# Turning the last batch of a GRU stream by VectorE and an exchange on GpSimd's queue, and moving one split behind the last sum

## The chip, the core and the metric

The kernel runs on one NeuronCore of one Trainium2 chip. The metric is the device time of one execution in microseconds (us), as the median of several runs; lower is better. The engines are TensorE (PE in the profile, its weight loads PEld), VectorE (DVE), ScalarE (ACT), GpSimd (POOL) and SyncE (SP). SyncE and GpSimd also issue transfers; each engine works off its own queue in order.

## The reference

The input is 16 graphs (batches) of 1024 nodes with 128 features, `x`, and a 0/1 adjacency matrix for each, `adj`. Two layers follow each other, each with a residual:

```python
h = jnp.maximum(_layernorm(x), 0.0)
for i in range(4):                                  # layer 0: gated
    hw = einsum('bnc,cd->bnd', h, weight[i])
    m = einsum('bjn,bjd->bnd', adj, hw)             # sum over neighbours
    h = _gru_cell(m, h, w_ih[i], w_hh[i], b_ih[i], b_hh[i])
x = x + h * mask
h = jnp.maximum(_layernorm(x), 0.0)
for i in range(4):                                  # layer 1: convolutions
    h = relu(einsum('bnm,bmc->bnc', adj, h @ W[i]) + b[i])
    mu, var = mean and variance of h over all batches and nodes
    h = gamma[i] * (h - mu) * rsqrt(var + EPS) + beta[i]
x = x + h
```

The GRU cell forms r and z with a sigmoid, n = tanh(xn + r * hn), and h = (1 - z) * n + z * h.

## The kernel before, in words

**Layout.** A batch is cut into eight blocks of 128 nodes and, for the gates, into two halves of 512 nodes. The gates work with features on the partitions (tile h, 128 x 1024). The sum over neighbours wants nodes on the partitions, split into a high part[...] and the low rest (two tiles, ghw in layer 0, chw in layer 1), so that each sum is done with two products for each row block (`aggregate_rows`, L520 to L530: 8 blocks x 2 parts x 2 halves = 32 products of 512 columns).

**Layer 0.** Two streams run against each other: `sa` does the even batches, `sb` the odd ones. In a half step (`half_step`, L1095) one stream does its sum over neighbours on TensorE while the other does its gates on ScalarE and VectorE. The order in this layer is written out by hand for every engine until the last half step; the calls under L1283 keep it by hand for TensorE, GpSimd and SyncE alone, and the rest, layer 1 included, is put in order by a scheduler that lets instructions of the two layers mix on each queue. After a sum, `agg_rows` (L947) copies the two halves from PSUM to the tiles m on ScalarE (L955, remembered as `last_m`); then `products` (L976, L993) does the gate products, `reset_gate`, `candidate` and `update_gate` the ScalarE and VectorE part, `less` and `mixed` the last of h (L1029, L1033, L1034).

**From features to nodes.** Between steps h is turned from features to nodes on the partitions in two moves: VectorE transposes 32 x 32 blocks (`half_out`, L719, into a tile t_h or t_out), and an exchange through DRAM puts the blocks where they belong (`exchange_out`, L588; `exchange_in`, L594; `pair_in`, L600, for both halves at once). The transfers go on SyncE's queue. `half_away` (L891) does this for each half as soon as it is ready. At the end of a batch (i + 1 - hf == L) it does so only if its stream has another batch (`self.b + 2 < B`), and `finish` (L1039) then fetches the pair back into the old h tile.

**The last two batches.** Batch 14 (stream sa) and batch 15 (stream sb) have no successor. `finish` calls `last_tail` (L757), and `tail_sums` (L726) turns h by eight transposes on TensorE (L735, tile pt_x), then adds it to x with the mask on VectorE (L741, one instruction for each block) and takes the statistics of the second layer norm (L664, L665). `last_tail` stores x (xmid, L752) on GpSimd's queue; its `rest` later normalizes (L680, y_mid) and stores that (ymid, L755). For batch 14 that is called after the last gates of batch 15, for batch 15 in the first convolution.

**Layer 1, first convolution.** `load_adjT` (L1303) brings the transposed adjacency of a batch from DRAM on SyncE's queue, as bfloat16 (L1308: tile block for even batches, packed for odd ones), and widens it to the rows wide (L1311 ScalarE for blocks 1, 4 and 7, L1313 VectorE for the others). `first_split` (L1366) loads y of a batch on GpSimd's queue (L1368), copies it to the high part on ScalarE (L1370) and subtracts for the low part on VectorE (L1371). The high and low tiles of even batches use the same memory as ghw of stream sa, those of odd batches that of stream sb, so a split waits for the last sum that read them. The sums of even batches are pc_m, of odd ones pc_g_r and pc_g_z. `row_sums` (L1402, pt_deg) counts neighbours once for batch 0, and `first_weights` (L1374, pw) applies the weight to a finished sum. `fetch_x` (L1426) brings part of x back early into weight tiles that are no longer used (w_hhT, w_mT), on GpSimd's queue too.

Of the kernel before, what the change touches and what calls it, by code (L numbers as in the profile page):

```python
# [17 lines left out]
HALF = 512  # L18
# [323 lines left out]
def exact_path(  # L342
# [21 lines left out]
    nc = tc.nc  # L364
    B, N, C = x.shape
    L = g_weight.shape[0]
    NB = N // P
    NH = N // HALF
# [13 lines left out]
    def tmp(name):  # L382
        return ps_t.tile([P, HALF], F32, tag="tmp", name=name)
# [5 lines left out]
    def flat(name):  # L389
        return keep.tile([P, NB, C], F32, tag="x", name=name, bufs=4)  # L390
# [4 lines left out]
    def half_tile(name):  # L395
        return keep.tile([P, N], BF16, tag="half", name=name, bufs=8)
# [4 lines left out]
    def hw_tiles(b, name):  # L401
        return [keep.tile([P, N], F32R, tag=f"hw{b % 2}{s}", name=f"{name}_{s}") for s in range(2)]
# [61 lines left out]
    turned = {}  # L464
# [68 lines left out]
    with ExitStack() as st:  # L533
# [51 lines left out]
                k = b * NB + j  # L585
                nc.scalar.activation(junk, lows, AF.Copy, accum_out=low[:, k : k + 1])

        def exchange_out(t, name, d=None):  # L588
            if d is None:
                d = rawd.tile([P, HALF], F32, tag="cross", name=f"cross_{name}", bufs=8)  # L590
            nc.sync.dma_start(d, t)
            return d

        def exchange_in(d, t):  # L594
# [2 lines left out]
            for s in range(4):  # L597
                nc.sync.dma_start(t[s * 32 : (s + 1) * 32, :].rearrange("r (t x) -> r t x", t=4), src[s])

        def pair_in(d, t):  # L600

            src = d.rearrange("h (t r) (s x) -> s r (h t) x", t=4, s=4)
            for s in range(4):
                nc.sync.dma_start(t[s * 32 : (s + 1) * 32, :].rearrange("r (a x) -> r a x", a=8), src[s])

        def look(b, row, j, part=0):

# [76 lines left out]
        def norm_stats(xt, name):  # L684
            nt = norm_tiles(name)
            norm_sums(xt, nt, range(NB))
            return nt

        def norm_apply(xt, y, nt):
            norm_root(nt, 0, NB)  # L690
            norm_scale(nt, 0, NB)
            norm_blocks(xt, y, nt, range(NB))
# [13 lines left out]
        def by_nodes(cols):  # L706
            return cols.rearrange("c (q k i) -> c k q i", q=4, i=32)

        def four_ways(cols):
            return cols.rearrange("p (k a c) -> p k a c", a=4, c=32)  # L710

        def blocks_out(src, name):

            d = rawd.tile([NH, P, HALF], F32, tag="pair", name=f"pair_{name}", bufs=4)
            for hf in range(NH):
                half_out(cross_tile(f"t_{name}_{hf}"), src, hf, name, d[hf])
            return d

        def half_out(t, src, hf, name, d=None):  # L719
            turned = nc.vector.transpose(by_nodes(t), four_ways(src[:, hf * HALF : (hf + 1) * HALF]))  # L720
            return exchange_out(t, f"{name}_{hf}", d), turned

        def cross_tile(name):
            return half_tile(name).bitcast(F32)

        def tail_sums(b, xt, hT, parts=None):  # L726

            for hf in range(NH):
                if parts:
                    pt = by_nodes(parts[hf])  # L730
                else:
                    pt = tmp(f"pt_x{b}_{hf}")
                    for q in range(BH):
                        k = hf * BH + q
                        nc.tensor.transpose(pt[:, q * P : (q + 1) * P], hT[:, k * P : (k + 1) * P], ident)  # L735
                    pt = four_ways(pt)
                for q in range(BH):
                    k = hf * BH + q
                    xk = xt[:, k, :].rearrange("p (a c) -> p a c", a=4)
                    mask = maskT[:, b * NB + k : b * NB + k + 1]  # L740
                    nc.vector.scalar_tensor_tensor(xk, pt[:, q, :, :], mask, xk, ALU.mult, ALU.add)  # L741
            return norm_stats(xt, f"mid{b}")
# [5 lines left out]
        def y_mid(b):  # L748
            return work.tile([P, N], F32, tag="h", name=f"y_mid{b}", bufs=7)

        def store_xmid(b, xt):
            nc.gpsimd.dma_start(xmid_d[b].rearrange("(k p) c -> p k c", p=P), xt)  # L752

        def store_ymid(b, y):
            nc.gpsimd.dma_start(ymid_d[b], y)  # L755

        def last_tail(b, xt, hT):  # L757
            nt = tail_sums(b, xt, hT)
            y = y_mid(b) if b + 1 < B else xt.rearrange("p k c -> p (k c)")
            store_xmid(b, xt)  # L760

            def rest():
                norm_apply(xt, y, nt)
                store_ymid(b, y)

            return rest
# [3 lines left out]
        class Stream:  # L770
# [119 lines left out]

            def half_away(self, hf):  # L891

                if self.i + 1 - hf == L and self.b + 2 < B:
                    if hf == 0:
                        self.pair = rawd.tile([NH, P, HALF], F32, tag="pair", name=f"pair_out{self.b}", bufs=4)
                    half_out(cross_tile(f"t_out{self.b}_{hf}"), self.new, hf, f"out{self.b}", self.pair[hf])
                elif self.turned_away(self.i + 1 - hf):
                    nm = f"{self.b}_{self.i + 1 - hf}"
                    out, self.last_dve = half_out(cross_tile(f"t_h{nm}_{hf}"), self.new, hf, f"h{nm}")
                    self.outs.append(out)  # L900
# [138 lines left out]
            def finish(self):  # L1039

                if self.i < L:
                    return
                args = self.b, self.xt, self.hT
                self.b, self.i = self.b + 2, 0
                if self.b >= B:
                    self.rest = last_tail(*args)
                    return
                self.take()
                ins, outs, h_in = self.next_ins, self.pair, self.hT
                parts = [args[-1][:, hf * HALF : (hf + 1) * HALF] for hf in range(NH)]  # L1050

                last = args[-1]
                at(clock[0] + 1, "ins", lambda: pair_in(ins, h_in))
                at(clock[0] + 1, "outs", lambda: pair_in(outs, last))
                self.plan(clock[0], (*args, parts))
# [3 lines left out]
        def at(n, place, go):  # L1059
            agenda.setdefault((n, place), []).append(go)  # L1060
# [91 lines left out]
        sa, sb = Stream(0), Stream(1)  # L1152
# [188 lines left out]
    def conv_input(b, i, aff, parts=1):  # L1341
        hT = work.tile([P, N], F32, tag="h", name=f"bn{b}_{i}", bufs=3)
        for k in range(parts):
            cols = slice(k * N // parts, (k + 1) * N // parts)
            nc.scalar.activation(hT[:, cols], feat[b][:, cols], AF.Identity, bias=aff[1], scale=aff[0])
        return hT

    def conv_hw(b, i, hT):
        hw = hw_tiles(b, f"chw{b}_{i}")
        for g in range(NH):  # L1350
            features_times(w_c[:, i, :], hT, hw, g, f"c{b}_{i}")
        return hw
# [13 lines left out]
    def first_split(b):  # L1366
        yt = flat(f"y{b}").rearrange("p k c -> p (k c)")
        nc.gpsimd.dma_start(yt, ymid_d[b])  # L1368
        hw = hw_tiles(b, f"chw{b}_0")
        nc.scalar.copy(hw[0], yt)  # L1370
        nc.vector.tensor_sub(hw[1], yt, hw[0].bitcast(F32))  # L1371
        return hw

# [76 lines left out]

    stats = small.tile([P, B * NH, 6], F32, tag="bn_st", name="stats0")
    hw, waiting = first_split(0), None
    for b in range(B):
        rows = load_adjT(b, 0)
        hw_next = first_split(b + 1) if b + 1 < B else None
        pm = banks(b, 0)
        aggregate(pm, hw, rows, 0)
        if waiting:
            last = first_weights(*waiting, stats)
            if b == 1:  # L1460
                with tc.issue_after(last.ins):
                    sb.rest()
        if b == B - 1:
            hw_next = raw_split(1)
        aggregate(pm, hw, rows, 1)
        if b == 0:
            row_sums(rows)
        hw, waiting = hw_next, (b, pm)
# [3 lines left out]
    for i in range(1, L):  # L1472
# [7 lines left out]
        hw = conv_hw(1, i, conv_input(1, i, aff, 2))  # L1480
        aggregate_rows(pm0, hw0, rows, range(6, NB))
        for b in range(1, B):
# [19 lines left out]
            hw = hw_next  # L1502
# [9 lines left out]
    for b in range(B):  # L1512
        hT = work.tile([P, N], F32, tag="h", name=f"bn{b}_{L}", bufs=3)
# [69 lines left out]
```

## Time and profile before

| what | value |
|---|---|
| median of 3 runs (lowest, highest) | 1788.07 us (1785.47, 1794.2) |
| the profiled execution's own time | 1789.26 us |
| its span, first to last instruction | 1787.5 us |
| TensorE busy, matmuls | 1759.3 us (98%) |
| VectorE, ScalarE, GpSimd busy | 1305.9, 1107.6, 379.3 us |
| granted TensorE clock, mean | 0.999 |
| gates of batch 14 on TensorE | 1137.25 to 1147.77 us |
| sum of batch 15 on TensorE | 1147.77 to 1155.47 us |
| transposes and gates of batch 15 | 1155.47 to 1166.64 us |
| first convolution, batch 0 | 1166.64 to 1175.17 us |
| batch 1, with row sums and weights | 1175.17 to 1188.12 us |

The times within the span count from its first instruction. A line of the timeline gives start, duration, engine, source line, operation, tile written and tiles read, shape and number of instructions, and in brackets how long the engine was idle before it and what ended that. Matmuls overlap in the pipeline, so the difference of two starts says more of TensorE's pace than the duration does: 0.23 us for a product of 512 columns with a high or low part, 0.86 us for two passes of a gate product.

### The profile page before, as it was taken

To read this page: it belongs to the slowest core of one execution; us is meant where nothing else is said; L and a number is where in the kernel's file an instruction comes from. 1 tells how busy PE (TensorE), PEld (TensorE's weight loads), DVE (VectorE), ACT (ScalarE), POOL (GpSimd) and SP (SyncE) were. 2 spreads that over 40 slices of the span, in tenths; PEclk is the share of its full clock that TensorE was granted. 3 is DMA by queue.
4 is the path that set the end of the run, shared out by engine and by line. 5 is a ranking of instruction groups with operands and counts; after the bars stand their busy time and mean duration, and the time that the engine had idled before them with its cause. 6 is when DMAs were issued, how large, how long until landed. Compare 5 with 4: busy or idle time off the path is not lost. (4 is left out here: it accounts for less than half of the span.)

```text
span 1787.5 us, 22335 instructions
## 1 busy us (share of the span) xinstructions
PE 1759.3 (98%) x6734; PEld 1191.7 (67%) x6734; DVE 1305.9 (73%) x2310; ACT 1107.6 (62%) x1713; POOL 379.3 (21%) x417
## 2 busy tenths in 40 slices
PE   9999999999999999999999999999999999999997
PEld 6565655565656565556555556577778888888886
DVE  7677877887887787887797787676666666666665
ACT  5356556556566556665655655476777767768765
POOL 4314323332331331422432333010100000000011
PEclk9999999999999999999999999999999999999999
DMA  7467657777676676776756768788766575767667
GB/s 259 135 175 262 189 163 272 179 208 241 204 200 213 223 212 197 245 202 202 260 169 186 265 174 227 256 287 311 271 228 241 207 253 201 245 224 245 238 217 268
DMA packets 363617, 400.16 MB, mean 224 GB/s; under 512 B 158188, under 2 KB 239888, under 8 KB 363488
## 3 DMA queue, kind: packets, MB, share of 16 engines
q1 hardware_dynamic: 342736, 323.59, 57.6%
q0 software_dynamic: 20224, 74.80, 11.3%
q8 instruction: 55, 0.90, 0.2%
q14 instruction: 74, 0.61, 0.1%
q10 hardware_dynamic: 528, 0.26, 0.0%
HBM read 267.47 MB, written 97.52 MB: 204 GB/s over the span
## 5 line engine op out<-in xcount | busy, mean ns | idle before, releaser
L524 PE MATMUL pm<-row,ghw 128*128 128x512 f32 x2048 | 503.6, 402 | 0.7 <-DVE ghw L926 0.6
L524 PEld LDWEIGHTS pm<-row,ghw 128*128 128x128 f32 x2048 | 383.8, 188 | 106.6 <-issue 29.2
L1016 ACT ACTIVATE r<-r,vecs 128x512 f32<-128x512 f32 x128 | 92.6, 723 | 255.0 <-DVE r L1013 253.1
L524 PE MATMUL pc_m<-wide,chw 128*128 128x512 f32 x1024 | 245.3, 395 | 0.0
L615 POOL CAST half<-row 128x1024 bf16<-128x1024 f32 x128 | 147.4, 1161 | 361.1 <-DMA adjT<-half 347.9
L524 PEld LDWEIGHTS pc_m<-wide,chw 128*128 128x128 f32 x1024 | 190.4, 188 | 41.9 <-issue 3.8
L524 PE MATMUL pc_g_r<-wide,chw 128*128 128x512 f32 x464 | 186.9, 403 | 0.3 <-ACT chw L501 0.3
L524 PE MATMUL pc_g_z<-wide,chw 128*128 128x512 f32 x464 | 181.0, 390 | 0.0
L577 POOL CAST row<-stage 128x1024 fp32r<-128x1024 f32 x112 | 128.6, 1156 | 243.7 <-DMA stage<-in_adj_dram 232.2
L1012 DVE SCALAR_TENSOR_TENSOR r<-g_hn,vecs,r 128x512 f32<-128x512 f32 x128 | 93.3, 729 | 117.9 <-ACT r L1011 66.9
L955 ACT COPY m<-pm 128x512 f32<-128x512 f32 x128 | 68.4, 585 | 163.5 <-PE pm L524 163.5
L1313 DVE CAST wide<-block 128x1024 fp32r<-128x1024 bf16 x160 | 109.9, 692 | 75.5 <-PE pc_m L524 48.3
L1313 DVE CAST wide<-packed 128x1024 fp32r<-128x1024 bf16 x160 | 110.1, 691 | 71.9 <-PE pc_g_z L524 53.5
L1311 ACT CAST wide<-packed 128x1024 fp32r<-128x1024 bf16 x96 | 100.6, 1048 | 58.5 <-PE pc_m L524 29.7
L993 PE MATMUL g_r<-m,w_mT 128*128 128x512 f32 x256 | 132.0, 597 | 3.4 <-ACT m L955 2.9
L1311 ACT CAST wide<-block 128x1024 fp32r<-128x1024 bf16 x96 | 100.7, 1049 | 53.9 <-PE pc_g_z L524 27.7
L993 PE MATMUL g_z<-m,w_mT 128*128 128x512 f32 x256 | 130.7, 592 | 0.0
L993 PE MATMUL g_xn<-m,w_mT 128*128 128x512 f32 x256 | 130.7, 592 | 0.0
L1361 DVE BATCH_NORM_STATS2 stats<-feat 128x6 f32<-128x512 f32 x128 | 84.1, 686 | 47.0 <-ACT feat L1360 45.9
L1029 DVE TENSOR_TENSOR h<-h,r 128x512 f32<-128x512 f32 x96 | 83.8, 872 | 41.9 <-ACT r L1016 41.8
L1033 DVE TENSOR_TENSOR h<-h,z 128x512 f32<-128x512 f32 x128 | 107.8, 842 | 6.8 <-ACT z L1020 0.2
L1011 ACT ACTIVATE r<-g_r,brz 128x512 f32<-128x512 f32 x128 | 87.9, 686 | 39.1 <-PE g_r L993 38.8
(186 smaller groups left out, 2830.5 us busy)
## 6 DMA issues: line engine op xcount, KB each, us to landing
block<-adjT_d SPq DMA_DIRECT2D x256, 256.0 KB, 4.7
packed<-adjT_d SPq DMA_DIRECT2D x256, 256.0 KB, 5.5
stage<-in_adj_dram SPq DMA_DIRECT2D x120, 512.0 KB, 5.7
adjT_d<-adjT POOLq DMA_DIRECT2D x16, 2048.0 KB, 7.7
cross_h<-t_h SPq DMA_DIRECT2D x92, 256.0 KB, 2.2
n_h<-cross_h SPq DMA_DIRECT2D x368, 64.0 KB, 2.0
xmid_d<-x POOLq DMA_DIRECT2D x16, 512.0 KB, 6.9
y<-ymid_d POOLq DMA_DIRECT2D x16, 512.0 KB, 5.4
```

The source lines that it names most:

```text
L524: nc.tensor.matmul(pm[hf], hw[s][:, j * P : (j + 1) * P], rows[j][:, hf * HALF : (hf + 1) * HALF], start=(j == 0 and s == 0), stop=(j == N ...
L577: nc.gpsimd.tensor_copy(t, stage[j % 4])
L615: nc.gpsimd.tensor_copy(t, row.bitcast(F32))
L993: nc.tensor.matmul(po, wT[:, i, g * C : (g + 1) * C], rhs, start=start, stop=stop)
L1011: nc.scalar.activation(r, pr, AF.Sigmoid, bias=brz[:, 3 * i : 3 * i + 1])
L1012: nc.vector.scalar_tensor_tensor(r, phn, b_hn(i), r, ALU.add, ALU.mult)
L1016: nc.scalar.activation(self.r, self.r, AF.Tanh, bias=b_in(self.i))
L1029: nc.vector.tensor_sub(ho, hin, self.r)
L1033: nc.vector.tensor_mul(ho, ho, self.z)
L1311: nc.scalar.copy(r, t)
L1313: nc.vector.tensor_copy(r, t)
L1361: nc.vector.bn_stats(stats[:, b * NH + hf, :], dst)
```

## The change

There are two edits, both at the passage from layer 0 to layer 1.

First, `half_away` also turns the two halves of the last batch of stream sa (batch 14) by VectorE, into t_out, and sends them to DRAM, on GpSimd's queue. `last_tail` of that stream then fetches them back into the h tile with four transfers, on GpSimd's queue too, and `tail_sums` adds from that tile in place of a PSUM tile, so that the eight transposes of batch 14 on TensorE are no longer made. Batch 15 stays as it was.

Second, the copy of the high part in `first_split` is put into `tc.issue_after(sb.last_m.ins)`: the scheduler may not place it before the last copy of m of stream sb (batch 15). It bears on the batches 0 and 1, whose copies would otherwise come earlier.

```diff
-        def exchange_out(t, name, d=None):
+        def exchange_out(t, name, d=None, eng=nc.sync):
...
-            nc.sync.dma_start(d, t)
+            eng.dma_start(d, t)
...
-        def pair_in(d, t):
+        def pair_in(d, t, eng=nc.sync):
...
-                nc.sync.dma_start(t[s * 32 : (s + 1) * 32, :].rearrange("r (a x) -> r a x", a=8), src[s])
+                eng.dma_start(t[s * 32 : (s + 1) * 32, :].rearrange("r (a x) -> r a x", a=8), src[s])
...
-        def half_out(t, src, hf, name, d=None):
+        def half_out(t, src, hf, name, d=None, eng=nc.sync):
...
-            return exchange_out(t, f"{name}_{hf}", d), turned
+            return exchange_out(t, f"{name}_{hf}", d, eng), turned
...
-        def last_tail(b, xt, hT):
-            nt = tail_sums(b, xt, hT)
+        def last_tail(b, xt, hT, outs=None):
+            parts = None
+            if outs is not None:
+                pair_in(outs, hT, nc.gpsimd)
+                parts = [hT[:, hf * HALF : (hf + 1) * HALF] for hf in range(NH)]
+            nt = tail_sums(b, xt, hT, parts)
...
-                if self.i + 1 - hf == L and self.b + 2 < B:
+                if self.i + 1 - hf == L and (self.b + 2 < B or self is sa):
+                    eng = nc.sync if self.b + 2 < B else nc.gpsimd
...
-                    half_out(cross_tile(f"t_out{self.b}_{hf}"), self.new, hf, f"out{self.b}", self.pair[hf])
+                    half_out(cross_tile(f"t_out{self.b}_{hf}"), self.new, hf, f"out{self.b}", self.pair[hf], eng)
...
-                    self.rest = last_tail(*args)
+                    self.rest = last_tail(*args, self.pair if self is sa else None)
...
-        nc.scalar.copy(hw[0], yt)
+        with tc.issue_after(sb.last_m.ins):
+            nc.scalar.copy(hw[0], yt)
```

In the changed program as built, TensorE's queue has eight instructions fewer (pt_x14), GpSimd's has six transfers more (two stores of t_out, four loads of h), and VectorE's has two transposes more. The copies of chw of the batches 0 and 1 stand on ScalarE behind the copies of m of batch 15. The scheduler has also put other things in another order: on SyncE, two transfers of the second block tile now come before the eight of packed; on ScalarE, the copy of chw of batch 2 now comes before the eight instructions y_mid of batch 14; on TensorE, the sixteen products of the row sums come after batch 1's sum and no longer in its middle, and the transposes of batch 15 stand some products later in batch 0's sum.

## The prediction, made before the changed kernel was run

> **What bounds the kernel now.** I read the page first. TensorE is busy in all but 28 us of the span of 1787.5 us, so only what makes TensorE's queue shorter, or makes it wait, can move the end.
>
> ```profile
> PE 1759.3 (98%) x6734; PEld 1191.7 (67%) x6734; DVE 1305.9 (73%) x2310; ACT 1107.6 (62%) x1713; POOL 379.3 (21%) x417
> ```
>
> Next the waits of TensorE alone (total us, times, longest): none is large, but one is what the last edit addresses, a gate product waiting for the copy of a sum out of PSUM.
>
> ```profile
> PE g_z L993 <- ACT z L1020: 5.0, 8, 0.7
> ...
> PE g_r L993 <- ACT m L955: 2.9, 4, 1.0
> ```
>
> All that the diff touches runs at one place, the passage from the first layer to the second, 1130 to 1190 us; the order of the changed program, as built, differs elsewhere by only one exchange of two neighbours (below). So I read the timelines there (start, duration, engine, line). TensorE:
>
> ```profile
> 1137.25 1.02 PE L993 MATMUL g_r<-h,w_hhT 128*128 128x512 f32 x2
> 1138.62 1.13 PE L993 MATMUL g_r<-m,w_mT 128*128 128x512 f32 x2 [0.34 <-ACT m L955]
> 1139.58 1.02 PE L993 MATMUL g_hn<-h,w_hhT 128*128 128x512 f32 x2
> ...
> 1155.47 1.03 PE L735 MATMUL pt_x<-ident,h 128*128 128x128 f32 x8
> 1156.34 1.02 PE L993 MATMUL g_r<-h,w_hhT 128*128 128x512 f32 x2
> ...
> 1166.64 0.60 PE L735 MATMUL pt_x<-ident,h 128*128 128x128 f32 x4
> 1166.99 3.46 PE L524 MATMUL pc_m<-wide,chw 128*128 128x512 f32 x14
> ```
>
> The reader is to see that TensorE is gapless but for 0.34 us, and that the eight transposes of batch 14 take 0.87 us of its queue (1155.47 to 1156.34). ScalarE shows why the gap is there: the copy of chw (batch 0) was let go before the copies of m and ran first.
>
> ```profile
> 1137.04 1.05 ACT L1370 CAST chw<-y 128x1024 fp32r<-128x1024 f32 x1 [6.04 <-PE pm L524]
> 1137.99 1.07 ACT L955 COPY m<-pm 128x512 f32<-128x512 f32 x2
> ...
> 1170.38 3.19 ACT L680 ACTIVATE y_mid<-x,ms_mid,rs_mid 128x128 f32<-128x128 f32 x8 [0.94 <-DVE ms_mid L676]
> 1174.92 1.05 ACT L1370 CAST chw<-y 128x1024 fp32r<-128x1024 f32 x1 [1.34 <-PE pc_m L524]
> 1176.28 1.05 ACT L1311 CAST wide<-packed 128x1024 fp32r<-128x1024 bf16 x1 [0.30 <-PE pc_g_z L524]
> ```
>
> Last, SyncE's queue and the table of transfers (us to landing): packed goes out before the second block.
>
> ```profile
> 1144.45 6.62 SPq L1308 DMA_DIRECT2D packed<-adjT_d  x8
> 1152.56 4.59 SPq L1308 DMA_DIRECT2D block<-adjT_d  x8
> ```
> ```profile
> pair_out<-t_out SPq DMA_DIRECT2D x28, 256.0 KB, 5.2
> ...
> h<-pair_out SPq DMA_DIRECT2D x56, 128.0 KB, 4.5
> ```
>
> [...]
>
> **The change part by part.** Negative is time won.
>
> (1) chw of batch 0 behind the last m. The product that read m started 1.37 us after the one before it (1137.25 to 1138.62), the next 0.96 later; the pace without a wait is 0.86. That is 0.51 + 0.10: **-0.61**. The two copies now run on ScalarE after m of batch 15, some 1156.0 to 1158.0; first user is the convolution's product after 1165, so this is covered, unless by what follows in (3).
>
> (2) The pt_x14 transposes go: **-0.87**. Added on VectorE are two t_out of 0.71; removed before them is the low part of chw (1.22), which moves later. The eight sums for x14 now read SBUF: 37.6 us over 112 is 0.34 each, 2.7 for eight, against 2.3 from PSUM (4.6 over 16).
>
> (3) VectorE's queue ahead of batch 15's last gates. As built, SyncE now issues two transfers of the second block before packed, and they wait until block's last casts are done (about 1152.2, as before, when 1152.56 was that wait). Packed 0 so goes out at 1153.2 instead of 1144.45, with two of 256 KB ahead of it; I take its landing as 1157, four us after issue as for the first block (1140.42 to the cast at 1144.52), bounds 1156 and 1159. VectorE, with t_out out of the way by 1153.9, stands at the cast of packed 0 till then. Behind it in order: that cast 0.60, chw low of two batches 2 x 1.2, scalar_tensor_tensor 0.65, cast 0.60, add 0.60: 1161.9. Tanh 0.7 on ScalarE, then h-r, h*z, the second scalar_tensor_tensor (1.9 together): 1164.6. Eight sums of x14 2.7, a statistic 0.2, h+r 0.6: h of the first half is ready at 1168.1. TensorE, 1.48 us ahead of the old time, starts the convolution at 1165.16, does seven products at 0.2275 and comes to pt_x15 at 1166.75: it **waits 1.35**. Then transposes 0.45, sixteen products 3.64, to 1172.2; the second half's add, tanh, and three operations with statistics between end about then. Transposes 0.45, nine products 2.05, the flag 0.15: batch 0 ends at 1174.85. The stage lasted 8.53 (1166.64 to 1175.17) and lasts 9.69: **+1.16**. Bounds -0.3 (no wait) and +3.2 (packed at 1159).
>
> (4) ScalarE's queue after it. As built, chw of batch 2 now stands before the eight y_mid and wide 4 behind them; before, y_mid was done while ScalarE would have waited. Chw 2 waits for batch 0's last high product, about 1174.4; +1.05, +3.19, +1.05: wide 4 is ready at 1179.7. TensorE wants it after sixteen products, 1174.85 + 3.64 = 1178.5: **waits 1.2**. The row sums that before stood in the middle of that batch (16 products, 3.75) now follow it, so nothing fills the gap. Thirty-two products 7.28, row sums 3.75, two weight products 1.71, and 1.2: 13.94 against 12.95 before (1175.17 to 1188.12): **+0.99**. Bounds 0 and +2.
>
> (5) The exchange itself, on GpSimd's queue. Two stores of 0.55 issue each, four loads of about 0.6 (between the 0.55 of a load of 128 rows and the 0.91 of one with 1024 pieces), then y2, y3 and x14's store queued behind. Second t_out at 1153.9; store landed after 3.3 (rows: 2.8 to 8.3 for w_hhT in this stretch): 1157.2; last load issued 1.8 later, landing 4.5 (pair_out's row): 1163.5. VectorE asks at 1164.6: covered, **0**. Y2 then lands near 1166, wanted at 1174.4; y3 and the x store have more room. Packed 6 and 7 wait for the two stores, since they share buffers; they are wanted after 1178. Bound above: 8.3 for the store is +4 after that cover.
>
> (6) At the second convolution four products (hw_c2) trade places with two of batch 1: nothing is removed, 0; bounds 0.3 either way, the only wait of a product on ScalarE's chw in TensorE's list.
>
> Sum: -0.61 - 0.87 + 1.16 + 0.99 = **+0.7 us**. The profiled execution took 1789.26 (span plus 1.76 around it), so 1789.9 on its own; on the median of the runs, 1788.07, it is **1788.7**. From 1188 us on TensorE has no gap, so what is won or lost there stays to the end.
>
> **Rivals.** *Faster*: packed lands by 1156 and ScalarE's order costs nothing; then only (1) and (2) count, with up to 0.5 of idle that the old stages had: -1.5 to -2.0, 1786.3. For it: VectorE was idle 0.6 at 1155.5 and the DMA share fell to 0.77 just before. Against: the order in (4) is fixed in the program. *Slower*: the exchange lands late. VectorE stands in order at x14's first sum, behind it h+r, behind that TensorE's pt_x15. It decides from 1164.6 on; each us later adds one. With store 5.2 and loads 4.5 plus 1.8 it lands at 1165.4; with the store at 8.3, at 1168.5: +0.8 to +4 more, so 1789.5 to 1793; I take 1791.5. For it: the pieces are 512 bytes and share the DMA engines with block and packed, which filled them (share 0.93 to 1.04 in these stages). *No effect as said*: ruled out for both edits by the order as built. An order elsewhere that hurts: left as 0.04.
>
> **How the numbers follow.** Main case 0.50; faster 0.23; exchange late 0.23; something else, either sign, 0.04. The runs before spread from 1785.47 to 1794.2, wider than any case, and a bound of 0.5% (8.9 us) is about what a measurement of this kernel can tell from no change. The range takes in both rivals but for the outer end of the slow one: 1785.2 to 1792.8. All three cases lie within 0.5%, so same 0.95; faster 0.02, slower 0.03 are the rest, as the late exchange has no bound in the rows but needs 8 us past its cover.
>
> **What would show it.** In the changed profile: no "ACT m" wait before the product at 1138 and the next step 0.86 after it; no pt_x<-h of batch 14; VectorE idle until "DMA packed" near 1154 to 1157; TensorE idle at pt_x15 on h (about 1.3) and at the fifth row of batch 1 on "ACT wide" (about 1.2); no VectorE idle before x14's sums. I am wrong if TensorE passes either place without waiting, or if VectorE waits there for h<-pair_out.

## The result, and the profile after

The changed kernel takes 1803.45 us in the median of 5 runs (1801.01 to 1804.12), the kernel before, beside it, 1789.79 us (5 runs, 1785.47 to 1794.2): a ratio of 1.0067, 95% interval 1.0054 to 1.0079. The forecast was 1788.7, its range ended at 1792.8. The profiled execution took 1803.86 us, its span is 1802.0.

The page first. TensorE has eight instructions fewer and 2.4 us more of busy time; the mean granted clock is 0.995, before it was 0.999.

```profile
PE 1761.7 (98%) x6726; PEld 1191.7 (66%) x6726; DVE 1300.5 (72%) x2312; ACT 1107.3 (61%) x1713; POOL 381.8 (21%) x423
```

TensorE's waits (total us, times, longest). The three lines are new: none of them is in the profile before. Each happens once, and all lie in the passage between the layers.

```profile
PE pt_x L735 <- DVE h L1039: 7.7, 1, 7.7
PE pc_g_r L524 <- ACT wide L1316: 1.1, 1, 1.1
PE pt_deg L1413 <- DVE ones_r L1454: 0.7, 1, 0.7
```

TensorE's timeline there:

```profile
1167.13 1.02 PE L998 MATMUL g_z<-m,w_mT 128*128 128x512 f32 x2
1167.59 2.16 PE L524 MATMUL pc_m<-wide,chw 128*128 128x512 f32 x7
1177.42 1.11 PE L735 MATMUL pt_x<-ident,h 128*128 128x128 f32 x4 [7.68 <-DVE h L1039]
1178.19 6.27 PE L524 MATMUL pc_m<-wide,chw 128*128 128x512 f32 x16
...
1192.04 0.50 PE L524 MATMUL pc_g_r<-wide,chw 128*128 128x512 f32 x1 [1.12 <-ACT wide L1316]
...
1196.66 3.92 PE L1413 MATMUL pt_deg<-wide,ones_r 128*128 128x512 f32 x16 [0.65 <-DVE ones_r L1454]
```

TensorE does its seven products as forecast and then stands for 7.68 us, not 1.35, at batch 15's first transposes. The sixteen products after that take 6.27 us; at the pace of the kernel before (0.23 us for each) they would take about 3.8. The next view, windows of the same trace (PEclk is the column before the last two), tells why: the clock fell to half while TensorE stood (at 1173.0, 3.3 us after its last product), and stayed there after it went on.

```profile
1166.20:1174.40 8.20, 3.54 (x12) 1.89 (x10) 1.45 (x4) 0.69 (x1) 2.17 (x4) 0.92 1.01 297
1174.40:1177.42 3.02, 0.00 (x0) 0.00 (x0) 3.02 (x12) 0.00 (x0) 0.55 (x1) 0.50 1.04 416
1177.42:1182.00 4.58, 4.58 (x13) 3.80 (x14) 4.50 (x19) 2.00 (x2) 0.36 (x1) 0.50 0.66 255
```

TensorE waited for h, h for VectorE. VectorE's queue shows two stops, the first at packed, the second at the first sum of batch 14. The timeline names no releaser for the second, the view of the tile pair_out below does:

```profile
1155.66 0.71 DVE L720 STREAM_TRANSPOSE t_out<-h 128x512 f32<-128x512 f32 x1
1159.98 0.69 DVE L1318 CAST wide<-packed 128x1024 fp32r<-128x1024 bf16 x1 [3.60 <-DMA packed<-adjT_d]
...
1166.92 0.74 DVE L1017 SCALAR_TENSOR_TENSOR r<-g_hn,vecs,r 128x512 f32<-128x512 f32 x1
1174.39 2.19 DVE L741 SCALAR_TENSOR_TENSOR x<-h,maskT,x 128x128 f32<-128x128 f32 x8 [6.72 <-issue]
```

What it waited for is on GpSimd's queue: the second store of the exchange, the four loads behind it. The view of the tile pair_out from 1155 us on then gives who waited for these five transfers, and their time from issue to landing.

```profile
1156.67 0.54 POOL L591 DMA_DIRECT2D pair_out<-t_out  x1 [5.86 <-DVE t_out L720]
1163.47 2.70 POOL L604 DMA_DIRECT2D h<-pair_out  x4 [6.27 <-DMA pair_out<-t_out]
```
```profile
  DVE x L741: 6.7, 1
...
DMA to landing us min/median/max: 5.7/6.1/8.6
```

The store landed 6.1 us after its issue, at about 1162.8; the loads after 5.7 to 8.6, the last at about 1174.2; VectorE went on at 1174.39. SyncE meanwhile kept the DMA engines full (DMA share 1.01 and 1.04 in the windows above) with transfers of 256 KB:

```profile
1155.22 7.94 SPq L1313 DMA_DIRECT2D packed<-adjT_d  x8
1163.21 2.80 SPq L1313 DMA_DIRECT2D block<-adjT_d  x6
```

**A ruler.** The median of the kernel before moves by a few us from run to run, with nothing different in the passage. So beside every median I give the *stretch*, from the start of the last pair of gate products g_z of layer 0 to the end of TensorE's last product, in the profiled execution. It is 612.0 us before and 624.7 after: +12.7. The waits make 7.68 + 1.12 + 0.65 = 9.45 of it. The clock, half from the restart at 1177.42 to about 1183.3, costs half of 5.8 us, 2.9. That is 12.4 of the 12.7. What steps (1) and (2) won lies ahead of the stretch.

### The profile page after: what moved, and what is told of

Its sections match the earlier page's. It is cut to its first block, busy times and chain, and to the rows that moved or that the text cites. A ratio compares the mean times of both kernels' runs of the same rounds, so it can differ in the third digit from the quotient of the medians.

```text
span 1802.0 us, 22329 instructions
## 1 busy us (share of the span) xinstructions
PE 1761.7 (98%) x6726; PEld 1191.7 (66%) x6726; DVE 1300.5 (72%) x2312; ACT 1107.3 (61%) x1713; POOL 381.8 (21%) x423
```

## The experiments

Two theories. **T1**: the exchange costs everything; it lands late, TensorE stands, and the clock falls. **T2**: the moved copy and the new queue orders ((3), (4)) cost most. Every kernel was timed beside the kernel before. "Ratio" is against that kernel on the same chip, with its 95% interval (it is taken from the single runs and isn't exactly the quotient of the two medians); the diffs are against the changed kernel unless said otherwise.

| run | median us (before) | ratio | stretch, change | TensorE's waits in the passage, us |
|---|---|---|---|---|
| e1_exchange_only | 1803.17 (1790.34) | 1.0069 [1.0053, 1.0086] | +9.6 | 5.8, 1.1, 0.2 |
| e2_copy_only | 1790.27 (1790.34) | 0.9998 [0.9988, 1.0008] | +0.1 | 0.2 |
| e3_on_sync | 1793.22 (1790.34) | 1.002 [1.0012, 1.0029] | +3.8 | 1.1, 2.15 |
| e4_sums_behind_gates | 1800.48 (1790.34) | 1.0056 [1.0038, 1.0074] | +9.7 | 1.6, 5.2 |
| e10_no_wait | 1796.75 (1791.21) | 1.0025 [1.0012, 1.0037] | +4.0 | 0.3, 1.1, 2.1 |
| e5_packed_first | 1798.55 (1791.21) | 1.003 [1.0018, 1.0042] | +8.5 | 3.9, 1.1, 0.6 |
| e6_idle72 | 1806.72 (1791.21) | 1.0079 [1.0062, 1.0095] | +16.1 | 1.1, 3.2, 0.2 |
| e9_sync_no_late | 1794.94 (1791.21) | 1.0018 [1.001, 1.0027] | +3.0 | 2.8 |
| e11_in_place | 1792.77 (1791.1) | 1.0006 [0.9996, 1.0015] | 0.0 | none |
| e12_crowd_held | 1797.43 (1791.1) | 1.0041 [1.0027, 1.0055] | +7.0 | 1.1, 3.7 |
| e13_held_in_place | 1794.68 (1791.06) | 1.0022 [1.0012, 1.0031] | +4.7 | 2.8 |
| e14_in_place_again | 1790.98 (1791.06) | 0.9999 [0.9988, 1.0009] | +0.1 | 0.15 |

### Each edit alone: e1_exchange_only, e2_copy_only

The first leaves out the second edit; the second kernel is the one before with the second edit alone.

```diff
-        with tc.issue_after(sb.last_m.ins):
-            nc.scalar.copy(hw[0], yt)
+        nc.scalar.copy(hw[0], yt)
```

> Only the first edit (batch 14 by VectorE and the exchange on GpSimd's queue); the copy of chw is left where the kernel before has it. T1 (the late exchange holds up VectorE's queue, in which the sums of batch 14 stand ahead of gates of batch 15): in this build the sums stand ahead of the second half's h-r and no longer ahead of the first half's h+r, so the long wait of TensorE moves from the first to the second pt_x of batch 15; with the transfer landing near 1174 us and the second half's last three gate steps of about 4 us behind the sums, TensorE waits 6 to 10 us there and its granted clock falls after it: 1798 to 1804 us. T2 (the loss comes from the second edit and the order that it gives to ScalarE): 1787 to 1791 us, no wait of TensorE above 2 us.

> Only the second edit (chw's copy behind the last m); batch 14 is turned by TensorE as before. T1: nothing is left to be late, so -0.6 us for the copy that no longer stands ahead of m, and the mean within noise of the kernel before: 1787 to 1791 us, no wait of TensorE above 1.5 us in the passage. T2: the loss stays, 1799 to 1805 us.

The first edit alone costs what the change costs, the copy alone nothing that can be measured. In e1_exchange_only TensorE waits 5.78 us for h at the *second* half's transposes, and the granted clock is 0.50 from 1176.8 to 1183.65. Its stretch doesn't hold all of its loss: batch 15's gates, just ahead, take 11.4 us from the first product to the last g_z, against 9.4 before, with waits for m and r. The copy is cleared, but the queue orders are not: e1_exchange_only has both of them (VectorE waits 4.31 us for packed, TensorE 1.08 for wide), e2_copy_only neither, so they come with the exchange. How much of the loss is the late landing and how much the orders, the next runs have to tell.

### The same exchange on SyncE's queue: e3_on_sync

```diff
-                pair_in(outs, hT, nc.gpsimd)
+                pair_in(outs, hT)
...
-                    eng = nc.sync if self.b + 2 < B else nc.gpsimd
+                    eng = nc.sync
```

> The changed kernel with batch 14's exchange on SyncE's queue, as all the other batches have it. In this build the sums of batch 14 stand on VectorE ahead of the second half's h-r of batch 15, and the four loads stand on SyncE behind packed 0 to 3. T1 with GpSimd's queue as the cause of the lateness: the loads land by about 1165 us, before VectorE asks, and the time is 1787 to 1791 us. T1 with the crowd of transfers as the cause: they land at 1170 to 1174 us on this queue too, TensorE waits 4 to 9 us at the second pt_x of batch 15: 1793 to 1802 us. T2: 1799 to 1805 us whatever the landing.

The view of pair_out gives the four loads' time to landing, and TensorE's and VectorE's timelines what is left:

```profile
DMA to landing us min/median/max: 3.5/3.5/3.5
```
```profile
1178.27 0.50 PE L524 MATMUL pc_g_r<-wide,chw 128*128 128x512 f32 x1 [1.12 <-ACT wide L1316]
1183.90 3.88 PE L1413 MATMUL pt_deg<-wide,ones_r 128*128 128x512 f32 x16 [2.15 <-DVE ones_r L1454]
```
```profile
1183.58 0.23 DVE L1454 CAST ones_r<-ones 128x128 fp32r<-128x128 f32 x1 [3.31 <-DMA ymid_d<-y_mid]
```

The exchange is over at 1160.8, 3.8 us before VectorE's first sum (1164.54); the 7.7 us are gone, with the clock's fall. But two waits stay, and the time lies between the two cases of the expectation. The first wait is step (4)'s. The second was in nobody's sum: ones_r is a constant that reads no y, yet it waits until the store of batch 14's y has landed, which points to memory that it takes over from y (e11_in_place tests that). Batch 14's sums and the store of its y, in the kernel before and then here:

```profile
1156.10 2.16 DVE L741 SCALAR_TENSOR_TENSOR x<-pt_x,maskT,x 128x128 f32<-128x128 f32 x8 [0.60 <-PE pt_x L735]
1173.87 0.54 POOL L755 DMA_DIRECT2D ymid_d<-y_mid  x1 [6.23 <-ACT y_mid L680]
```
```profile
1164.54 2.18 DVE L741 SCALAR_TENSOR_TENSOR x<-h,maskT,x 128x128 f32<-128x128 f32 x8
1177.57 0.54 POOL L755 DMA_DIRECT2D ymid_d<-y_mid  x1
```

The sums start 0.8 us after the last g_z here (1163.70) and started 9.7 us before it in the kernel before (1165.78). So y is stored 13.9 us after that product, before 8.1; the store also takes 5.9 us to land, before 2.9; and what takes y's memory next is held up. I call this the **second chain**.

### VectorE not held by the sums: e4_sums_behind_gates

Batch 14's sums get their place behind the last gates of batch 15.

```diff
...
+            with tc.issue_after(sb.last_dve.ins):
+                rest = sa.rest()
             with tc.issue_after(sb.last_act.ins):
-                sa.rest()
+                rest()
```

> The changed kernel with the sums of batch 14 (x + h) kept on VectorE's queue behind the last gate step of batch 15; the exchange stays as late as it is. T1: TensorE's wait at the first pt_x of batch 15 falls from 7.7 to under 1.5 us and the clock stays up; of the loss of 13.7 us, 6 to 12 come back, the rest is a new wait of batch 1's sum for rows that VectorE widens behind batch 14's sums and statistics: 1790 to 1797 us. T2: nothing comes back, 1801 to 1805 us.

Missed: the transposes no longer wait, but y is later still, ones_r waits for its store, and TensorE stands 5.21 us before the row sums, which then take 6.17 us for sixteen at half the clock (0.50 from 1182.3 to 1189.1). The loss has moved from the first chain to the second.

### Nothing waits for the loads: e10_no_wait

All six transfers stay, but the loads go to a tile of their own, and the sums of batch 14 take h as it stands, with features where nodes belong: this kernel leaves batch 14's turning out of its result. The sums stay behind the second r of batch 15 by hand, but the scheduler now puts the last step of h of the first half ahead of them.

```diff
-                pair_in(outs, hT, nc.gpsimd)
+                pair_in(outs, y_mid(100), nc.gpsimd)
...
```

> The changed kernel with every transfer as it is, but the four loads land in a spare tile and the sums of batch 14 take h as it stands (features where nodes belong: batch 14's rows of the result are other ones), so that VectorE has no landing to wait for; the eight sums stand at the same place in its queue, behind the second r of batch 15. T1: the loss goes with the wait, no wait of TensorE above 1.5 us at the transposes of batch 15 and no fall of its clock: 1788 to 1791 us. T2 (order of ScalarE and SyncE) or a cost of the transfers' traffic by itself: the loss stays in part or whole, 1794 to 1803 us.

In between. TensorE's waits:

```profile
PE pt_deg L1419 <- DVE ones_r L1460: 2.1, 1, 2.1
PE pc_g_r L524 <- ACT wide L1322: 1.1, 1, 1.1
```

So the wait for the loads, with its clock and the place of the sums, carries 12.7 - 4.0 = 8.7 us of the stretch. Of the 4.0 that stay, 3.5 are the three waits in the table (0.3, 1.1 and 2.1), so the transfers going by cost at most half a us beside them; and e3's two waits are back, whichever queue the exchange is on. VectorE waits 3.44 us for packed here too, and TensorE no more than 0.27 at the transposes.

### packed before block: e5_packed_first

SyncE's order is put back as it was, so that VectorE doesn't wait for packed (step (3)).

```diff
...
+            if b == 2 and i == 0:
+                with tc.issue_after(sent[-1].ins):
+                    nc.sync.dma_start(t, adjT_d[b][j])
+            else:
+                sent.append(nc.sync.dma_start(t, adjT_d[b][j]))
```

> The changed kernel with one constraint on SyncE's queue: the block tile of batch 2 behind the eight packed of batch 1, as in the kernel before; every other queue is the same. If the two blocked transfers on SyncE are what throws packed and the exchange together (step 3 of the prediction grown large): packed is out by 1154 us, the second store lands in about 3 us, VectorE does not wait 3.6 us for packed, the loads land by 1167 us, TensorE's wait falls under 2 us: 1789 to 1793 us. If the exchange is late on GpSimd's queue whatever SyncE sends (batch 2's block is the crowd then): it lands at 1170 to 1174 us and TensorE waits 4 to 8 us: 1798 to 1803 us.

The order carries about a third of the loss: 4.2 us of the 12.7. VectorE passes packed, and the second store lands in 3.6 us instead of 6.1, so that the last load lands 3.3 us after the start of the last g_z instead of 7.1. But the loads still take 6.4 to 8.0 us, the last until about 1171.2, and TensorE still waits for h:

```profile
1174.47 1.11 PE L735 MATMUL pt_x<-ident,h 128*128 128x128 f32 x4 [3.90 <-DVE h L1039]
1175.24 5.89 PE L524 MATMUL pc_m<-wide,chw 128*128 128x512 f32 x16
```

### TensorE kept busy: e6_idle72

Seventy-two useless transposes stand where TensorE waited; the second half's transposes and the row sums are put in place by hand.

```diff
+            pt = tmp("pt_x15_0")
+            for k in range(72):
+                nc.tensor.transpose(pt[:, k % 4 * P : (k % 4 + 1) * P], sb.z[:, :P], ident)
...
```

> The changed kernel with 72 transposes of no use (of a finished z tile) on TensorE between the first products of batch 0 and the first pt_x of batch 15, about 8 us of work; the second pt_x is held behind the 24th product as before, and the row sums come ahead of batch 1's sum. The wait of VectorE stays as it is. If the half pace after the wait comes from TensorE having stood still: the granted clock stays above 0.9, the 28 products behind the first pt_x go at 0.23 us each, 6.4 us instead of about 9: 1799 to 1802 us. If the half pace has another cause (the load on memory at that time): the products stay near 0.39 us each, 1803 to 1805 us.

```profile
1170.04 8.08 PE L1322 MATMUL pt_x<-ident,z 128*128 128x128 f32 x72
...
1178.90 4.85 PE L524 MATMUL pc_m<-wide,chw 128*128 128x512 f32 x20
...
1190.44 0.80 PE L1444 MATMUL pt_deg<-wide,ones_r 128*128 128x512 f32 x1 [3.16 <-DVE ones_r L1485]
1191.48 6.20 PE L1444 MATMUL pt_deg<-wide,ones_r 128*128 128x512 f32 x15 [0.24 <-DVE x L1058]
```

The point it was made for came out: after 8 us of useless work the products keep 0.24 us each, at a granted clock of 1.00, where after 7.7 us of standing they took 0.39, at 0.50. So it is the standing that cost the clock. The total missed, 1806.72 us against at most 1805: the second chain bit again, with 3.16 us and then half the clock (0.50 from 1190.1 to 1196.9).

### ones_r out of the way: e9_sync_no_late

As e3_on_sync; ones_r gets memory of its own, and row 4 of batch 1 goes from ScalarE to VectorE (step (4)).

```diff
+    ones_r = feat_pool.tile([P, P], F32R, tag="ones_r", name="ones_r")
...
-            if j % 3 == 1:
+            if j % 3 == 1 and (b, i, j) != (1, 0, 4):
...
-    ones_r = work.tile([P, P], F32R, tag="ones_r", name="ones_r", bufs=1)
```

> The exchange on SyncE's queue as in e3, and two edits for the waits that its trace still showed: the tile ones_r in memory that no store still reads (TensorE waited 2.15 us for it at the row sums), and row 4 of batch 1 widened by VectorE in place of ScalarE (1.12 us). T1: both waits go and nothing follows: 1.5 to 3.3 us under e3's 1793.2, so 1789.5 to 1791.5 us. If the removed transposes (0.9 us) and the copy (0.6 us) count in full as well: 1788.5 to 1790 us. If other waits take their place: 1792 to 1794 us.

Both waits are gone, but one takes their place, and the time is above all three cases of the expectation. (ones_r itself stands on VectorE behind other work until 1187.15, when the store has landed, so this run doesn't show whose memory it had.) TensorE's single wait, and ScalarE's line behind it:

```profile
PE pw_g_hn L1388 <- ACT cm L1387: 2.8, 1, 2.8
```
```profile
1187.28 1.07 ACT L1387 COPY cm<-pc_m 128x512 f32<-128x512 f32 x2 [1.52 <-DMA ymid_d<-y_mid]
```

The tiles cm wait for that same store. The trouble isn't ones_r alone, it is the late y.

### y in place: e11_in_place, e14_in_place_again

As e3_on_sync with row 4 on VectorE; batch 14's y is written over its x, so that the late store holds no tile of layer 1.

```diff
-            y = y_mid(b) if b + 1 < B else xt.rearrange("p k c -> p (k c)")
+            y = xt.rearrange("p k c -> p (k c)")
```

> The exchange on SyncE's queue as in e3, with row 4 of batch 1 widened by VectorE and the normalized y of batch 14 written over its x in place of a tile of its own, so that ones_r and the cm tile of the first convolution no longer lie in memory that the late store of y reads. If the rest of e3's loss is that chain (late sums, late y, late store, memory kept): TensorE's waits at the row sums (2.15 us in e3) and at the first weights (2.79 us in e9) go, the stretch from the last gate product to the end falls from e3's 615.8 to 612 to 613 us, against 612.0 in the kernel before, and with the two savings ahead of it (1.5 us) the time is 1788 to 1790.5 us beside a kernel before of about 1790.5. If y over x waits for the store of x instead: TensorE waits again by 2 to 3 us, 1792 to 1795 us.

> The kernel of e11_in_place once more (exchange on SyncE, y of batch 14 over its x, row 4 of batch 1 by VectorE), now beside e13_held_in_place. Its stretch was that of the kernel before, and the two savings ahead of the stretch (0.6 and 0.9 us) should make it 1.5 us faster; its median was 1.1 us slower than before with an interval of 0.9996 to 1.0015. If that was scatter, 1788 to 1791, ratio 0.999 to 1.000; if something ahead of the stretch takes the 1.5 us, again 1.0005 to 1.001.

TensorE waits nowhere over 0.2 us in the passage, and the stretch is that of the kernel before: 612.0 and 612.1. ones_r, allocated as in e3_on_sync, is now made at 1180.74 in e11_in_place, 3.1 us before y's store is even issued (1183.88): what it had waited for was y's memory. The two chains, with step (4)'s wait, are the whole loss of the stretch. The 1.5 us of steps (1) and (2) don't show in the medians (+1.7 us, which missed the expectation, and -0.1 against the kernel before); their size is that of the scatter, so whether something ahead of the passage takes them stays open.

### The crowd taken away, GpSimd's queue kept: e12_crowd_held, e13_held_in_place

SyncE sends packed first, and may send its second block tile only after a transfer of 512 bytes that reads the first column of h and so waits for all four loads. The second of the two adds y in place and row 4 on VectorE.

```diff
+            if b == 2 and i == 0:
+                if j == 0:
+                    with tc.issue_after(sent[-1].ins):
+                        sent.append(nc.sync.dma_start(landed_d, sa.landed_h[:, :1]))
...
```

> The changed kernel, exchange on GpSimd's queue, with SyncE's queue in another order: packed of batch 1 first, then a transfer of 512 bytes that reads the fetched h and so waits for its landing, and only then the block tile of batch 2 and packed of batch 3. Memory is left to the exchange while the loads run. If the crowd is what makes the loads land late: they take 3 to 4.5 us (as on SyncE's queue) in place of 6 to 8.6, land by about 1167 us, and TensorE's wait at batch 15's transposes is under 1 us; the row sums may still wait 2 us: 1790.5 to 1794 us. If GpSimd's queue is slow by itself: 6 to 8 us again, TensorE waits 3 to 4 us and its clock falls: 1797 to 1800 us.

> The exchange stays on GpSimd's queue, with SyncE's large transfers held back until its first block has been fetched (as in e12_crowd_held), and now the y of batch 14 is written over its x and row 4 of batch 1 is summed by VectorE (as in e11_in_place), so that no tile of the second chain lies in memory that the late store of y still reads. If the passage is lengthened by two chains only, the crowded memory and the late y, both are gone here with the edit as it was made (GpSimd's queue): no wait of TensorE over 1 us between g_z and the row sums, the stretch from the last gate product of layer 0 to the end of the last product falls from 619.0 to 612-613 (before 612.0), time 1788 to 1792. If GpSimd's queue has a cost of its own, TensorE waits again and the stretch stays at 615 or more, time 1793 to 1798. If y written over x waits for the store of x, 2 to 3 us on the stretch.

The loads' time to landing in e12_crowd_held:

```profile
DMA to landing us min/median/max: 2.5/2.6/2.9
```

On the same queue, while SyncE sends nothing (from 1154.34 to 1162.87), they land in less than half the time, the last at about 1162.7, and VectorE doesn't wait for them. Beside e5_packed_first, which differs only in that SyncE may go on sending, this puts the late loads on the crowd. GpSimd's queue alone isn't the cause, nor is the crowd alone: on SyncE's queue, at a DMA share of 0.86, the loads took 3.5 us (e3_on_sync); with both, in the changed kernel, 5.7 to 8.6. Nor were they late where VectorE was busiest: while the loads of e12_crowd_held ran (1158.06 to 1162.73) VectorE was busy 4.51 of 4.67 us, and in the changed kernel, where they took up to 8.6 us, 4.03 of 10.74 (1163.47 to 1174.21). The time missed (1790.5 to 1794 was expected), since the second chain then shows in full (ones_r, 3.73 us, the clock at 0.50 from 1187.5 to 1190.9). e13_held_in_place removes that, and gets another form of it, the one that its expectation named last, and larger (4.7 us of stretch, not 2 to 3): SyncE's held transfers now go out from 1165.49 on, around the store of x, which takes 13.0 us to land (issued 1168.71), and y may not be written over x before that.

```profile
1181.84 3.19 ACT L680 ACTIVATE x<-x,ms_mid,rs_mid 128x128 f32<-128x128 f32 x8 [4.72 <-DMA xmid_d<-x]
```
```profile
1186.50 1.93 PE L1401 MATMUL pw_g_hn<-cm,w_c 128*128 128x512 f32 x2 [2.78 <-ACT cm L1400]
```

TensorE waits for neither transposes nor ones_r, but 2.78 us at the weights. With the exchange on SyncE's queue the same store landed in 7.5 and 7.7 us (e11_in_place, e14_in_place_again) and held nothing.

## Why the prediction was wrong, step by step

- **(1), chw behind the last m, -0.61: right.** The wait for m is gone and the step is 0.86; 0.61 won.
- **(2), the eight transposes gone, -0.87: right,** 0.90 measured. Neither can be told in a median.
- **(3), VectorE's queue, +1.16: the wait was right, its price can't be told.** VectorE did wait for packed, 3.60 us where the working has 3.1 (1153.9 to 1157). In the changed kernel the longer wait for the loads hides what that costs TensorE; in e10_no_wait, where nothing waits for the loads and a step of h stands ahead of the sums, it is 0.27. What the working didn't have is that the same order on SyncE also delays the exchange (e5_packed_first, 4.2 us of stretch).
- **(4), ScalarE's order, +0.99: right.** The wait for wide was forecast as 1.2 and measured as 1.12. That y_mid, now behind chw of batch 2, is stored later too, and what waits for y's memory, was not followed.
- **(5), the exchange "covered, 0": the step that failed.** The store was priced at 3.3 us from w_hhT<-xmid_d (the median of three that were issued from 1091.4 to 1166.2, 2.8 to 8.3) and the loads at 4.5 from pair_out's rows on SyncE's queue, both medians over other stages; they took 6.1 and 5.7 to 8.6, in a stage where the prediction itself noted a DMA share of 0.93 to 1.04. From the end of the second t_out to the last landing the working has 9.6 us (1153.9 to 1163.5); it took 17.8 (1156.4 to 1174.2). VectorE asked at 1167.66, so it stood 6.7 us, where the working had 1.1 to spare. The first store landed in 2.2 us, at a DMA share of 0.59, the second in 6.1, at 1.01; with the crowd held back (e12_crowd_held) the loads took 2.5 to 2.9. What in the crowd delays GpSimd's transfers, no run here shows.
- **(6), order elsewhere, 0: right;** the stretch of e11_in_place is 612.0.
- **The slow rival named the mechanism:** late landing, VectorE in order at batch 14's first sum, h and pt_x15 behind it, from 1164.6 on. That each us late costs one held for the wait itself: VectorE stood 6.72 us for the loads, and TensorE's wait grew from the forecast 1.35 to 7.68, by 6.33. But the bound of +4 was too small, and it left out two things. The clock fell to 0.50 during that wait and stayed there for 5.8 us of the work after it, 2.9 us more. And it treated the sums' lateness as ending at pt_x15, while the second chain runs on through y, its store and the memory of ones_r and cm. Even with the exchange on time, that chain costs 2.15 us of waiting (e3_on_sync) to 3.73 (e12_crowd_held).

The range ended at 1792.8 since it took +4 as a bound, though the text said that the late exchange "has no bound in the rows". The medians stand up to about 3 us above what the stretch and the two savings give (after: +13.7 against 12.7 - 1.5 = 11.2; e11_in_place: +1.7 against -1.5); whether that is scatter between executions, later landings in the ones not profiled, or something in layer 0 that takes the savings, the runs don't tell.

## What to carry to other kernels

Price a transfer by the traffic in its own stage, not by a median over the kernel, and if the DMA share is already 1.0 there, leave its landing unbounded in the range (the second store, at 1.01, took 6.1 us where 3.3 was priced). When work moves from a full engine to a route through memory, follow what comes later because of it to the end: not only the next reader, but every store, and every tile that will take the stored tile's memory. The waits of TensorE of 3.16 us and more in this passage, and one of 2.78, cost more than their length, since the clock fell to 0.50 and came back only 3.6 to 6.4 us after work had gone on.

## What the runs showed of the hardware

**The clock.** TensorE kept its full pace after standing 2.1 and 2.15 us (e10_no_wait, e3_on_sync: the sixteen products of the row sums behind the wait took 3.92 and 3.88 us) and, once, 2.79 us (e9_sync_no_late: granted clock 1.00 from 1183 to 1195). It went to half the clock with 2.78 (e13_held_in_place), 3.16 (e6_idle72), 3.7 (e12_crowd_held), 3.9 (e5_packed_first), 5.2 (e4_sums_behind_gates), 5.8 (e1_exchange_only) and 7.7 us (the changed kernel). Why 2.78 us cost the clock and 2.79 didn't, these traces don't show. How long the half clock lasted, from its fall to its return, in the changed kernel, e5_packed_first and e13_held_in_place, read from narrow windows of their traces:

| run | half clock from, to (us) | length, us | granted clock in it | TensorE's work went on at |
|---|---|---|---|---|
| after (the changed kernel) | 1173.03, 1183.27 | 10.24 | 0.50 | 1177.42 |
| e5_packed_first | 1172.66, 1179.49 | 6.83 | 0.50 | 1174.47 |
| e13_held_in_place | 1186.69, 1190.11 | 3.42 | 0.50 | 1186.50 |

In the other four traces with a fall the clock was at 0.50 for 6.8 us (e1_exchange_only, e4_sums_behind_gates, e6_idle72) and 3.4 (e12_crowd_held). In the seven it came back 3.6 (e13_held_in_place) to 6.4 us (e6_idle72) after work had gone on. It fell 3.3 us after the last product in the changed kernel, 2.1 in e5_packed_first, and 3.0 in e13_held_in_place, where work had gone on again for 0.2 us.

**Landing.** Loads of 128 KB on GpSimd's queue took 2.5 to 3.0 us while SyncE sent nothing (e12_crowd_held, e13_held_in_place) and 4.4 (e6_idle72) to 8.6 (the changed kernel) beside its transfers; on SyncE's own queue in the same stage 3.5 (e3_on_sync) to 5.7 (e14_in_place_again).
